# Gated units: turned rows placed a step earlier, moments and norms issued tile by tile

## The chip, the cores and the metric

The kernel runs on one core of one Trainium2 chip. A core has five engines that run side by side and wait for each other through semaphores: TensorE (PE in the profile; its weight loads are listed as PEld), VectorE (DVE), ScalarE (ACT), GpSimd (POOL) and SyncE (SP), which here issues most of the DMAs. The metric is the device time of one execution in microseconds (us); the time of a kernel is the median of several executions.

## What is computed

The reference takes x of shape (2, 2048, 256) in float32 and adds two sublayers to it, each between layer norms. The first is an attention of three branches. The second is a stack of two layers, and it is the one that matters here:

```python
def _layer(x, wqkv, qs, ksc, wo, lg, lb, w1, b1, w2, b2):
    h = shift_token(x)                      # second half of the channels from the token before
    q, k, v = split(h @ wqkv)               # 8 heads of 64
    q, k = rotary_xpos(l2norm(q) * qs, l2norm(k) * ksc)
    x = x + local_attention(q, k, v) @ wo   # window of 128, one window back
    h = shift_token(x)
    mu, var = h.mean(-1), h.var(-1)
    h = (h - mu) / sqrt(var + 1e-05) * lg + lb
    a, g = split(h @ w1 + b1)               # 682 columns each
    x = x + (a * gelu(g)) @ w2 + b2
    return x
for l in range(2):
    x = _layer(x, ...)
```

The change touches the last five lines of a layer, which the kernel calls the gated units.

## The kernel before

**Tiling.** A tile is 128 tokens (on the 128 partitions) by 256 channels; there are 16 tiles in each of the 2 batches. Four tiles (GT) make a group, so there are 8 groups, X[g] holds the input and Y[g] the running value of a group in SBUF. Attention runs tile by tile, 32 a layer, the batches taking turns. The gated units run group by group, 8 a layer, the batches taking turns too (GORDER). The 682 hidden columns are cut into six chunks (NCH): five of 128 and one of 42.

**An order written out by hand.** Nothing is reordered by a planner. Every piece of work is put on a list with a place (`put(place, f, ...)`), the list is sorted by place, and the functions are called in that order. Each engine carries out its own instructions in the order of the calls. A tile of attention comes every 12400 places (TILE), a chunk of the gated units every 5170 (STEP). A place is only a rank: an instruction starts when its engine has come to it and what it waits for is done. Where an item and a chunk have the same step, the chunk's products come first (offset 0), then its gate (offset 10), then the item (offset 20).

**A gated group.** For group i the steps count from its first chunk. `shift` (step -9) brings the second half of the channels down by one token: two DMAs on SP's queue from Y into `sh`, one more for row 0 from the last token of the group before (`kept`, copied by POOL; for the first group of a batch POOL writes zeros). `moments` (step -6) takes mean and variance of the four tiles (`stats`: two L149 and one L150 on VectorE a tile) and the inverse deviation (`rstd_of`, L155 and L156 on POOL). `normed` (steps -4 and -3) writes the normed halves `hn` (L160, four a half, VectorE); with the second half POOL adds the second bias to Y (L1036). `turned` (steps -2 and -1) turns a half with four TensorE transposes into one PSUM bank (L1042) and scales it into `hT` (L1043, VectorE). `inner` (steps 0 to 5) multiplies hT by a chunk of w1 (L1051): a gate product and a value product, each over two halves of the contraction; the last, narrow chunk has both in one. `gate` takes the Gelu on ScalarE (L1069) and the product with the value on VectorE (L1070) into `u`. `back` (steps 6 to 9, beside the next group's chunks 0 to 3) multiplies u by w2 (L1077) and adds to Y (L1079). In the second layer `closing_moments` and `closing_norm` follow half a step and one and a half steps after each back, and SP stores the rows (L1092).

**Where stages meet.** The gated units of a layer start before its attention ends: step 0 of group 0 stands 28150 places after the start of the last tile, and until place 37400 after it no Gelu is called. So the last tiles' attention (L924 divides the probabilities, L934 turns them, L976 sums the two parts of the output, L981 projects it, L810, L821, L828, L832 and L836 prepare queries and keys) stands among the first two groups' shifts, moments, norms and turns. `sh` and attention's output `oT` share two buffers; so do attention's `rr` and the gated units' hn and hT (`hh`). PSUM has two banks each for pa and pb and four for pc. The place of the steps is in one line, and it is what the change edits:

```python
plan += [(-9, shift), (-6, moments), (-4, normed, 0), (-3, normed, 1), (-2, turned, 0), (-1, turned, 1)]
...
for i, g in enumerate(GORDER):
    for c in range(NCH):
        place = base + (NCH * i + c) * STEP
        put(place, inner, g, c, ...)
        put(max(place, no_gate_until) + 10, gate, g, c)
    for at, f, *arg in plan:
        put(base + (NCH * i + at) * STEP + 20, f, g, *arg)
```

## Time and profile before

| what | us |
|---|---|
| median of 3 runs (1682.47 to 1685.27) | 1682.78 |
| the profiled execution | 1687.03 |
| its span, first to last instruction | 1685.3 |
| TensorE clock granted, mean | 0.98 of full |
| gated units, first layer: from one group to the next in mid-stage | 31.50 |
| L1051, product of a chunk with w1, one instruction (mean) | 0.61 |
| L1042, transposes in the gated units, one (mean) | 0.28 |
| L1043, scaling of a turned half, one (mean) | 0.81 |
| L160, norm of a half tile, one (mean of each half) | 0.34 and 0.43 |

A span runs from the first to the last instruction that the profiler saw; 1.7 us of the profiled execution lie around it. In the timelines, matmuls are pipelined: consecutive ones overlap, so the time from one start to the next says more than a duration. The slices of the span show the stages:

```profile
PE   5999985699999999879999999999999997999998
DVE  2555566478888788843333336888888885344443
POOL 6401245575665666611110146666666662123322
```

Each digit is the busy share of an engine in one of 40 equal slices of 42 us, in tenths. Slices 0 to 6 are the first sublayer; 7 to 16 attention of the first layer and 17 to 22 its gated units; 23 to 33 and 34 to 39 the same of the second layer. In the gated units TensorE is nearly always busy and VectorE and GpSimd are not. In attention three engines are busy.

### The profile page before, as it was taken

The numbers are of one execution on the slowest core, as the hardware profiler recorded it, in microseconds if no ns is written. First come the engines' busy times: TensorE is split into PE (matmuls) and PEld (weight loads), VectorE is DVE, ScalarE is ACT, GpSimd is POOL, SyncE is SP. The second block draws the span as 40 slices with busy tenths as digits, with TensorE's granted clock in tenths as the row PEclk, the third lists the DMA queues.
The fourth block names the chain that finished last, engine by engine and source line by source line (L and its number), as shares of the span: only waits on it lengthen the run. The fifth ranks groups of instructions, "written<-read, shape, count | busy, mean of one in ns | idle before, by whom it ended". The sixth has DMA issues, their size and how long they took to land.

```text
span 1685.3 us, 32263 instructions
## 1 busy us (share of the span) xinstructions
PE 1560.2 (93%) x12255; PEld 1034.6 (61%) x12255; DVE 1044.4 (62%) x3084; ACT 757.7 (45%) x2201; POOL 748.2 (44%) x932
## 2 busy tenths in 40 slices
PE   5999985699999999879999999999999997999998
PEld 4966763266666666645555556666666664555555
DVE  2555566478888788843333336888888885344443
ACT  3334364367677677531111125767767763111110
POOL 6401245575665666611110146666666662123322
PEclk9999997899999999999999999999999998999999
DMA  6000000200000000011000001000000000000000
GB/s 204 2 1 1 1 1 0 78 8 5 8 8 6 8 8 8 6 47 26 9 7 16 0 32 29 8 8 5 8 8 5 10 3 13 8 24 27 26 26 25
DMA packets 31674, 30.40 MB, mean 18 GB/s; under 512 B 4344, under 2 KB 29792, under 8 KB 31520
## 3 DMA queue, kind: packets, MB, share of 16 engines
q1 hardware_dynamic: 27264, 25.17, 4.7%
q10 hardware_dynamic: 3200, 2.63, 0.5%
q8 instruction: 97, 1.59, 0.4%
q0 software_dynamic: 1056, 0.55, 0.4%
q14 instruction: 57, 0.47, 0.1%
HBM read 19.95 MB, written 4.19 MB: 14 GB/s over the span
## 4 chain that ended last, share of the span: by engine, by line
PE 71%; DVE 5%; ACT 1%; POOL 1%; DMA 1%; issue 1%; POOLq 0%; SPq 0%; DVEq 0%; ACTq 0%
PE pa L794 18%; PE pc L1077 10%; PE pa L1051 9%; PE pb L1051 7%; PE pb L981 6%; PE pb L934 5%; PE pc L954 5%; PE pc L887 5%; PE pb L844 3%; PE pc L1051 1%; DMA sh<-Y 1%; DVE hh L1043 1%; DVE u L1070 1%; DVE rr L810 1%; PE pb L772 1%; DVE hh L160 1%
## 5 line engine op out<-in xcount | busy, mean ns | idle before, releaser
L794 PE MATMUL pa<-wqkv,h 128*128 128x512 f32 x768 | 373.6, 609 | 21.6 <-ACT h L776 10.3
L821 POOL TENSOR_TENSOR rr<-rr 128x256 f32<-128x256 f32 x256 | 178.8, 732 | 301.2 <-DVE rr L810 267.1
L1069 ACT ACTIVATE ge<-pa,vcol 128x512 f32<-128x512 f32 x92 | 62.9, 686 | 384.8 <-PE pa L1051 384.8
L917 ACT ACTIVATE prob<-prob,off 128x192 f32<-128x192 f32 (+2 forms) x512 | 225.0, 443 | 15.4 <-DVE off L908 14.8
L794 PEld LDWEIGHTS pa<-wqkv,h 128*128 128x128 f32 x768 | 132.1, 192 | 134.2 <-issue 104.7
L155 POOL TENSOR_SCALAR r<-mv 128x1 f32<-128x1 f32 (+2 forms) x72 | 15.8, 219 | 446.2 <-DVE mv L150 445.4
L1051 PE MATMUL pa<-hh,w 128*128 128x512 f32 x368 | 182.3, 613 | 20.9 <-DVE hh L1043 15.6
L832 POOL TENSOR_TENSOR ss<-ss,mhalf 128x16 f32<-128x16 f32 x64 | 186.5, 2914 | 5.3 <-DVE den L922 4.0
L939 ACT COPY probT<-pb 128x384 f32<-128x384 f32 (+1 forms) x256 | 119.7, 468 | 149.0 <-PE pb L934 145.9
L1077 PE MATMUL pc<-w,u 128*128 128x256 f32 x768 | 176.3, 380 | 0.0
L1077 PEld LDWEIGHTS pc<-w,u 128*128 128x128 f32 x768 | 146.4, 191 | 46.1 <-issue 29.3
L810 DVE TENSOR_TENSOR rr<-pa,cs 128x1024 f32<-128x1024 f32 x128 | 150.5, 1215 | 19.4 <-POOL cs L765 14.4
L904 DVE CUSTOM_DVE_ANT_0 prob<-pc,mask_loc 128x192 f32<-128x192 f32 (+2 forms) x512 | 148.6, 345 | 19.9 <-PE pc L887 19.1
L1070 DVE SCALAR_TENSOR_TENSOR u<-pb,vcol,ge 128x512 f32<-128x512 f32 x73 | 54.7, 749 | 152.3 <-PE pb L1051 133.2
L1051 PE MATMUL pb<-hh,w 128*128 128x512 f32 x292 | 138.3, 596 | 0.0
L934 PE MATMUL pb<-ident,prob 128*128 128x128 f32 x752 | 119.7, 282 | 18.6 <-DVE prob L924 16.7
L934 PEld LDWEIGHTS pb<-ident,prob 128*128 128x128 f32 x752 | 90.7, 144 | 72.6 <-issue 39.9
L836 POOL TENSOR_TENSOR rr<-rr,ss 128x512 f32<-128x512 f32 x128 | 131.5, 1048 | 2.5
L924 DVE TENSOR_TENSOR prob<-prob,den 128x768 f32<-128x768 f32 x128 | 127.3, 995 | 5.0
L981 PE MATMUL pb<-wo,oT 128*128 128x256 f32 x512 | 122.9, 383 | 5.3 <-DVE oT L976 4.1
L801 ACT ACTIVATE sq<-pa 128x512 f32<-128x512 f32 x128 | 75.8, 592 | 94.6 <-PE pa L794 91.8
L887 PE MATMUL pc<-kr,qT 64*64 64x192 f32 (+2 forms) x2688 | 111.9, 290 | 3.6 <-ACT qT L848 3.3
(263 smaller groups left out, 2549.5 us busy)
## 6 DMA issues: line engine op xcount, KB each, us to landing
X<-_attn_hidden_states_dram SPq DMA_DIRECT2D x8, 512.0 KB
cs<-in_rope_dram SPq DMA_DIRECT2D x32, 128.0 KB
out_dram<-res SPq DMA_DIRECT2D x32, 128.0 KB
sh<-Y SPq DMA_DIRECT2D x16, 254.0 KB
w<-in_L_ffn_w_dram SPq DMA_DIRECT2D x6, 640.0 KB
wqkv<-in_L_ffn_wqkv_dram SPq DMA_DIRECT2D x2, 1536.0 KB
Wc<-in_L_attn_Wc_dram ACTq DMA_DIRECT2D x1, 1024.0 KB
wo<-in_L_ffn_wo_dram SPq DMA_DIRECT2D x2, 512.0 KB
```

The source lines that it names most:

```text
L794: nc.tensor.matmul(ps, lhsT=src, rhs=W[l]["wqkv"][:, h, j * INNER : (j + 1) * INNER], start=(h == 0), stop=(h == 1))
L810: nc.vector.tensor_tensor(s["rr"][:, j], ps, tab, ALU.mult)
L821: nc.gpsimd.tensor_tensor(dst, dst, rr[:, j, 1, :, hi : hi + hd], ALU.add)
L832: nc.gpsimd.tensor_tensor(S[n]["ss"], S[n]["ss"], mhalf, ALU.pow)
L836: nc.gpsimd.tensor_tensor(dst, dst, S[n]["ss"][:, j * HEADS : (j + 1) * HEADS].unsqueeze(2).to_broadcast([P, HEADS, DH]), ALU.mult)
L887: nc.tensor.matmul(ps[half][at : at + HALF, i, c : c + m], lhsT=s["qT"][lo : lo + DH, pair, half * HALF : (half + 1) * HALF], rhs=KR[b][lo ...
L904: nc.vector.tensor_tensor_reduce(out=p[:, i, half, lo:hi], in0=s["s", quad][half][:, i, lo:hi], in1=mask_loc[:, lo:hi], scale=1.0, scalar= ...
L917: nc.scalar.activation(ph, ph, AF.Exp, bias=s["off", quad][:, j : j + 1], accum_out=s["den", quad][:, j : j + 1])
L934: nc.tensor.transpose(pt[:, c, :], flat[:, c * P : (c + 1) * P], ident)
L981: nc.tensor.matmul(pz, lhsT=S[n]["oT"][:, i, :], rhs=W[l]["wo"][:, i, :], start=(i == 0), stop=(i == HEADS // 2 - 1))
L1051: nc.tensor.matmul(ps, lhsT=w1_s[:, h, lo : lo + P], rhs=s["hT"][:, h, :], start=(h == 0), stop=(h == 1))
L1077: nc.tensor.matmul(pz, lhsT=s["u"][:, c, k * P : (k + 1) * P], rhs=W[l]["w2"][:, c, :], start=(c == 0), stop=(c == NCH - 1))
```

## The change

`moments` is cut into four calls of one tile each, at steps -7, -6.78, -6.56 and -6.34; the inverse deviation stays at step -6 in a call of its own, `deviations`. `normed` is cut into eight calls of one tile and half, from step -4.5 to -2.96 at 0.22 of a step; the buffer `hh` is asked for in the first of them. The second bias is a call of its own at step -2.5. The two turns go from -2 and -1 to -2.1 and -1.1. With the offset of 20 places, -2 and -1 came just after the chunk of that step; -2.1 and -1.1 come 497 places ahead of it (0.1 of a step less the offset). `shift` stays at -9. No arithmetic is changed.

```diff
-        def moments(g):
+        def moments(g, k):
             s = G[g]
-            mv = small.tile([P, GT, 2], F32, tag="mv4", name="mv")
-            for k in range(GT):
-                stats(mv[:, k, :], Y[g][:, k, 0:P], s["sh"][:, k, :])
-            s.update(mv=mv, r=rstd_of(mv, GT, 1e-5))
-            hh = act.tile([P, 2, 2 * GT * P], F32, tag="rr", name="hh")
-            s["hn"] = hh[:, 0].rearrange("p (h k t) -> p h k t", h=2, k=GT)
-            s["hT"] = hh[:, 1].rearrange("p (h t) -> p h t", h=2)
-
-        def normed(g, h):
+            if k == 0:
+                s["mv"] = small.tile([P, GT, 2], F32, tag="mv4", name="mv")
+            stats(s["mv"][:, k, :], Y[g][:, k, 0:P], s["sh"][:, k, :])
+
+        def deviations(g):
+            G[g]["r"] = rstd_of(G[g]["mv"], GT, 1e-5)
+
+        def normed(g, h, k):
             s = G[g]
-            for k in range(GT):
-                norm(s["hn"][:, h, k, :], s["sh"][:, k, :] if h else Y[g][:, k, 0:P], s["mv"], k, s["r"])
-            if h:
-                nc.gpsimd.tensor_tensor(Y[g], Y[g], W[l]["b2"].unsqueeze(1).to_broadcast([P, GT, H]), ALU.add)
+            if "hn" not in s:
+                hh = act.tile([P, 2, 2 * GT * P], F32, tag="rr", name="hh")
+                s["hn"] = hh[:, 0].rearrange("p (h k t) -> p h k t", h=2, k=GT)
+                s["hT"] = hh[:, 1].rearrange("p (h t) -> p h t", h=2)
+            norm(s["hn"][:, h, k, :], s["sh"][:, k, :] if h else Y[g][:, k, 0:P], s["mv"], k, s["r"])
+
+        def second_bias(g):
+            nc.gpsimd.tensor_tensor(Y[g], Y[g], W[l]["b2"].unsqueeze(1).to_broadcast([P, GT, H]), ALU.add)
...
         plan = [(NCH + k, back, k) for k in range(GT)]
-        plan += [(-9, shift), (-6, moments), (-4, normed, 0), (-3, normed, 1), (-2, turned, 0), (-1, turned, 1)]
+        plan += [(-9, shift), (-6, deviations), (-2.5, second_bias), (-2.1, turned, 0), (-1.1, turned, 1)]
+        plan += [(-7 + 0.22 * k, moments, k) for k in range(GT)]
+        plan += [(-4.5 + 0.22 * (h * GT + k), normed, h, k) for h in range(2) for k in range(GT)]
```

## The prediction

> **What bounds the kernel now.** I read the page first (busy shares, slices), then who TensorE waits for, then the timelines of TensorE, VectorE, GpSimd and the DMA queue in a group of gated units in mid-stage and in the overlap where attention ends.

> ```profile
> PE 1560.2 (93%) x12255; PEld 1034.6 (61%) x12255; DVE 1044.4 (62%) x3084; ACT 757.7 (45%) x2201; POOL 748.2 (44%) x932
> ```

> and from the list of waits (total us, times, longest):

> ```profile
> PE pa L1051 <- DVE hh L1043: 15.6, 14, 1.2
> PE pb L981 <- DVE oT L976: 4.1, 3, 1.5
> ```

> TensorE is the bound, 93% busy. Of its waits only one comes back in every group: 14 times (groups 2 to 8 of each layer) the first gate product waits for L1043, the scaling that takes the turned rows out of PSUM. TensorE in a mid group:

> ```profile
> 882.29 1.88 PE L1051 MATMUL pa<-hh,w 128*128 128x512 f32 x4
> 884.00 1.88 PE L1051 MATMUL pb<-hh,w 128*128 128x512 f32 x4
> 885.72 0.60 PE L1042 MATMUL pc<-ident,hh 128*128 128x128 f32 x4
> 886.16 1.88 PE L1051 MATMUL pa<-hh,w 128*128 128x512 f32 x4
> 887.88 0.60 PE L1042 MATMUL pc<-ident,hh 128*128 128x128 f32 x4
> 888.31 1.02 PE L1051 MATMUL pa<-hh,w 128*128 128x512 f32 x2
> 890.44 1.12 PE L1051 MATMUL pa<-hh,w 128*128 128x512 f32 x2 [1.11 <-DVE hh L1043]
> 891.40 1.88 PE L1051 MATMUL pb<-hh,w 128*128 128x512 f32 x4
> ```

> Chunk 4 (two products), first turn, chunk 5 (one product), second turn, then the next group's chunk 0: its first half needs only the first turned half and runs, its second half waits. VectorE at that time:

> ```profile
> 886.66 0.80 DVE L1043 TENSOR_SCALAR hh<-pc,vcol 128x512 f32<-128x512 f32 x1
> 888.79 0.75 DVE L1070 SCALAR_TENSOR_TENSOR u<-pa,vcol,ge 42x512 f32<-42x512 f32 x1 [1.33 <-ACT ge L1069]
> 889.58 0.81 DVE L1043 TENSOR_SCALAR hh<-pc,vcol 128x512 f32<-128x512 f32 x1
> ```

> The second turn is done at 888.31, but its L1043 stands in VectorE's queue behind chunk 5's gate product, which waits for ScalarE. It ends at 890.39 and TensorE goes on at 890.44.

> In the overlap of layer one (676 to 767; layer two repeats it at 1362 to 1452) other things decide[...]. TensorE's waits there:

> ```profile
> 688.13 1.97 PE L981 MATMUL pb<-wo,oT 128*128 128x256 f32 x8 [1.08 <-DVE oT L976]
> 707.15 1.51 PE L934 MATMUL pb<-ident,prob 128*128 128x128 f32 x6 [4.25 <-DVE prob L924]
> 717.49 1.99 PE L981 MATMUL pb<-wo,oT 128*128 128x256 f32 x8 [1.50 <-DVE oT L976]
> ```

> VectorE's rows that stand before them, then GpSimd's, then the DMA queue's issue and VectorE's read of what it brings:

> ```profile
> 701.58 3.94 DVE L160 TENSOR_SCALAR hh<-sh,mv,r 128x128 f32<-128x128 f32 x4
> 744.12 2.78 DVE L924 TENSOR_TENSOR prob<-prob,den 128x768 f32<-128x768 f32 x1
> ```

> ```profile
> 702.84 2.34 POOL L1036 TENSOR_TENSOR Y<-Y,b 128x1024 f32<-128x1024 f32 x1
> ```

> ```profile
> 706.38 0.71 SPq L1016 DMA_DIRECT2D sh<-Y  x1
> ```

> ```profile
> 721.43 0.29 DVE L149 BATCH_NORM_STATS2 st<-sh 128x6 f32<-128x128 f32 x1 [0.21 <-DMA sh<-Y]
> ```

> Four norms that elsewhere take 1.10 us take 3.94, and L924 takes 2.78 for 0.96, each time beside POOL's second bias. The shifted rows (sh), issued from 705.59, are there at 721.4: some 15.8 us.

> [...]L924 ends 0.8 after L1036 does (746.09). [...]254 KB in 15 us is 17 GB/s, so I expect these 15 us wherever sh is issued. [...]After 4.25 us idle the six transposes at 707.15 take 1.51; the same six take 0.82 at 691.98.

> **The change part by part.**

> *Turns a step sooner.* Place -1.1 puts the second turn ahead of chunk 5, and its L1043 ahead of chunk 5's gate product on VectorE; the first one goes ahead of chunk 4. Take chunk 4's end as 0. Second turn until 0.43. VectorE has chunk 4's gate product from 0.27 to 1.02 (885.99 against 885.72), then L1043 from 0.94 to 1.75. TensorE needs it after chunk 5 (1.72) and the half product (0.86): at 0.43 + 1.72 + 0.86 = 3.01. It is 1.2 early; no wait is left. What goes: the product would have started at 888.31 + 0.86 = 889.17 and started at 890.44: 1.27, plus 0.10 since it restarts slower (0.96 to the next one instead of 0.86). 1.37 a group. Check: five chunks at 3.44, 1.72, four backs at 2.59 and two turns at 0.43 make 30.14; the groups stand 31.50 apart (854.82, 886.32, 917.82 in the chain of waits). 14 x 1.37 = 19.2 us off. In the second layer a closing norm (place -1.5), perhaps held by the second bias, delays L1043 by some 0.7: still 0.6 early.

> *Norms in pieces* (64 of each half, 0.34 us; none added). In mid-stage nothing waits for them. They straddle the shift of the next group (-9), so that sh's old buffer is still in use there and the other one is taken. In layer one the DMA queue then no longer waits for the norms of the group before (issue at 884.00, norms done 883.93): it can issue much sooner. The second bias (POOL, 2.35 us) starts as soon as the first half's last norm is done and nothing of POOL's own is ahead[...]; the gate product of chunk 3 behind it is asked for 3.44 + 0.27 after that back's sum and has over 5 us until its bank is needed: nothing. The buffer of hn and hT is asked for at the first norm instead of at the moments; the attention tiles that share it are asked for in the same order as before: nothing.

> *Moments a step sooner, in pieces* (each 0.63: two L149, one L150). They now come right after chunk 5's gate product. In layer two the sh DMAs stand behind an output store (1597.28, then 1597.70) and land at about 1614.1; The store waits for a closing norm that comes 0.5 sooner (two norms ahead of it instead of four, 0.26 apart), so 1613.6. VectorE gets to the moments at about 1607 and blocks there over 6 us. Queued behind: the gate products of chunks 0 and 1 and a back's sum. The moments end at 1613.6 + 0.46 + 3 x 0.63 = 1616.0, chunk 0's gate product (0.75) at 1616.7, which is 11.3 after the group's first product (1605.41). TensorE needs that bank for chunk 2's second product at 2 x (3.44 + 2.59) + 1.72 = 13.8. Cover 2.4; cost nothing, and beyond it one for one. The price of this wait is bounded by 0 (sh landed) and by the whole landing time; I take the trace's 15.8 to 16.4 from issue.

> *Overlap, tiles 27 and 28.* Four moments stood in a block at 683.80 ahead of L976. Two of them now fall into VectorE's wait for scores (0.70 at 679.73)[...]; L976 comes 1.0 sooner, and the stall of 1.08 at 688.13 mostly goes: 0.9 off a layer.

> *Overlap, group 1.* Its norms spread out and the second bias moves behind L832: the 4.25 stall (L924 behind four norms and L828) shortens by about 2. On POOL the order was L821, second bias, the copy for the next shift, L832 (2.9), L836; now it is L821, copy, L832, second bias, L836: L832 starts at about 703.6 instead of 705.98, but with 2.9 and 2.35 before it L836 starts at about 708.9, as before (708.96), and TensorE's turn of those rows waits for it. I count 0; bounds -2 and +2.35. The second turn now stands ahead of three transposes of probabilities and waits for a bank that L972 frees: under 0.2.

> *Overlap, group 2.* Its sh takes the buffer that L981 of tile 28 frees (702.5; 701.7 with the 0.9 gained) instead of that of the norms (705.52), so it lands at 701.7 + 15.9 = 717.6. But its first moments now stand ahead of tile 29's L976, which was at 716.76 in front of them: 717.6 + 0.46 + 0.68 puts L981 at 718.85 instead of 717.49: 1.36 later. In layer two the same sum gives 1404.1 for 1401.95: 2.15. In layer one the idle time before it grows to over 4 us, so TensorE may come back at half clock[...]; in layer two L981 is already slow there (3.41). After it three norms are ahead of time, and the second bias starts 0.85 sooner against L924: 0.85 off a layer, and 0.3 (no wait for tops in layer one).
> Layer one: 1.36 + 1.7 - 0.85 - 0.3 = +1.9; layer two 2.15 - 0.85 = +1.3. (The 0.9 is inside these.) Bounds for both together: -3.5 if sh lands before it is asked for[...].

> Sum: -19.2 + 3.2 = -16. The profiled execution was 1687.03 (span 1685.3), so 1671 for its like; the median of the runs shown is 1682.78, 4.2 lower, and gives **1667**. About 0.2% (3.4 us) is what a measurement of this kernel can tell from no change.

> **Rivals.** *The overlap gives, too* (sh is not late): -19.2 - 3.5 = -22.7, 1660. For: one block of moments visibly stalls L981. Against: 15.8 us of DMA. *The wait moves to the moments in mid-stage*: sh comes later than worked out and eats the cover of 2.4; at 0.5 to 1 us in each of ten groups, 5 to 10 back: 1674. For: five waits of 0.4 to 0.5 us on sh are there today a step later. *Slower*: the same DMA in layer two decides the group. Five groups (4 to 8) lose one for one beyond 2.4; they eat the 16 at 3.2 each, so from 5.6 us later than I have it; at 7 us it is 5 x 4.6 = 23, 1690. For: output stores and sh share a queue, and some stores take 7.5 us to issue. Against: sh is issued before those. *It doesn't do what it says*: L1043 stays behind a late gate product, 1682.

> **How the numbers follow.** Forecast 0.60 (its own range 1661 to 1672), overlap gives 0.12, mid-stage wait 0.14, slower 0.10, nothing 0.04. Leaving out the last two and the outer part of the third: 1659 to 1675. Faster 0.86, same 0.04, slower 0.10.

> **What would show it.** Right: groups 30.1 us apart in both layers, no wait of L1051 for L1043; in layer two waits of VectorE's L149 for sh of about 6 us; L981 near 718.9 waiting behind sh. Wrong: groups still over 30.5 apart, L1051's second product waiting for L1070, or a gap over 6 us before L981 of tile 29.

## The result and the profile after

| | before | after |
|---|---|---|
| median of 6 runs, us | 1684.31 (1682.47 to 1685.27) | 1667.32 (1665.84 to 1671.76) |
| profiled execution; its span, us | 1687.03; 1685.3 | 1667.55; 1665.8 |
| from group to group in mid-stage, us | 31.50 | 30.12 |

The ratio is 0.9903, 95% interval 0.989 to 0.9916: 17 us faster, where 1667 had been forecast. In the changed kernel every line from the second bias on is three higher: turns L1045, scaling L1046, products L1054, Gelu L1072, gate product L1073, back L1080, second bias L1039, store L1095.

The page's busy times first (busy us, share of the span, instructions):

```profile
PE 1559.2 (94%) x12255; PEld 1038.1 (62%) x12255; DVE 1054.1 (63%) x3084; ACT 757.0 (45%) x2201; POOL 748.3 (45%) x932
```

TensorE works as long as before (1560.2); what went is idle time. Its list of waits (total us, times, longest) no longer has L1054 waiting for L1046 at all, where L1051 waited 14 times for L1043. Something else has grown: before, L844 waited 2.4 us in all for L836. L934 has come down from 16.7.

```profile
PE pb L844 <- POOL rr L836: 9.9, 5, 3.7
PE pb L934 <- DVE prob L924: 9.4, 5, 2.9
PE pb L981 <- DVE oT L976: 4.5, 2, 2.4
```

TensorE in the same mid group as the one shown of before (start, us, engine, line, operation, tiles, count):

```profile
876.68 0.60 PE L1045 MATMUL pc<-ident,hh 128*128 128x128 f32 x4
877.11 1.88 PE L1054 MATMUL pa<-hh,w 128*128 128x512 f32 x4
878.83 1.88 PE L1054 MATMUL pb<-hh,w 128*128 128x512 f32 x4
880.55 0.60 PE L1045 MATMUL pc<-ident,hh 128*128 128x128 f32 x4
880.99 3.60 PE L1054 MATMUL pa<-hh,w 128*128 128x512 f32 x8
```

First turn, chunk 4, second turn, then eight products in one unbroken row: chunk 5 and both halves of the next group's chunk 0. And VectorE beside it:

```profile
880.82 0.75 DVE L1073 SCALAR_TENSOR_TENSOR u<-pb,vcol,ge 128x512 f32<-128x512 f32 x1 [2.54 <-PE pc L1045]
881.49 0.80 DVE L1046 TENSOR_SCALAR hh<-pc,vcol 128x512 f32<-128x512 f32 x1
883.62 0.75 DVE L1073 SCALAR_TENSOR_TENSOR u<-pa,vcol,ge 42x512 f32<-42x512 f32 x1 [1.33 <-ACT ge L1072]
```

L1046 now stands between chunk 4's gate product and chunk 5's. It ends at 882.29; TensorE comes to the half that needs it at 880.55 + 3.01 = 883.56, 1.3 us later.

In the overlap of layer one TensorE's waits have changed places:

```profile
702.62 0.85 PE L934 MATMUL pb<-ident,prob 128*128 128x128 f32 x6 [1.56 <-DVE prob L924]
...
708.61 1.12 PE L844 MATMUL pb<-ident,rr 128*128 128x128 f32 x4 [3.73 <-POOL rr L836]
710.40 1.11 PE L844 MATMUL pb<-ident,rr 128*128 128x128 f32 x4 [0.67 <-POOL rr L836]
711.44 2.64 PE L954 MATMUL pc<-probT,v 64*64 64x128 f32 x64
...
718.13 1.99 PE L981 MATMUL pb<-wo,oT 128*128 128x256 f32 x8 [2.37 <-DVE oT L976]
```

The stop of 4.25 us before L934 is down to 1.56, but 3.73 and 0.67 us of waiting for GpSimd's L836 stand right behind it, and L981 waits longer than before (1.50). GpSimd shows why L836 is no sooner: the second bias stands ahead of it.

```profile
701.53 3.71 POOL L832 TENSOR_TENSOR ss<-ss,mhalf 128x16 f32<-128x16 f32 x1
705.22 2.33 POOL L1039 TENSOR_TENSOR Y<-Y,b 128x1024 f32<-128x1024 f32 x1
707.52 2.83 POOL L836 TENSOR_TENSOR rr<-rr,ss 128x512 f32<-128x512 f32 x2
```

The same in the kernel before, whose execution is 0.7 us behind at the start of the overlap:

```profile
708.96 2.05 POOL L836 TENSOR_TENSOR rr<-rr,ss 128x512 f32<-128x512 f32 x2
```

To compare kernels, I cut the execution at TensorE's own instructions: the overlap from L981 of tile 25 to the first back of the third group (it holds three of the seven waits a layer), and mid-stage from there to the first back of the eighth group (the other four).

| us | overlap, layer 1 | mid-stage 1 | overlap, layer 2 | mid-stage 2 |
|---|---|---|---|---|
| before | 168.5 | 169.1 | 168.8 | 151.8 |
| after | 165.0 | 163.6 | 166.3 | 146.3 |

Mid-stage gives 4 x 1.375 in each layer. The overlaps should give 3 x 1.375 = 4.1; they give 3.5 and 2.6, so they cost 0.6 and 1.6 us. A last 1.6 us comes from the hand-over to layer two, where four projections run at full clock after and not before (1.98 us for 3.12). The stretch from the eighth group's first back to L981 of the fifth tile of layer two takes 81.0 to 81.1 us in eight of the fourteen profiled kernels and 82.7 to 82.8 in the other six, and kernels with the whole change stand among both. The pieces alone are among the eight, the turns alone among the six. The clock decides there, as the last section shows for six of them: this gain is not the change's.

### The profile page after: what moved, and what is told of

The parts are those of the page before. It is cut to its first block, busy times and chain, and to the rows that moved or that the text cites. A ratio compares the mean times of both kernels' runs of the same rounds, so it can differ in the third digit from the quotient of the medians.

```text
span 1665.8 us, 32261 instructions
## 1 busy us (share of the span) xinstructions
PE 1559.2 (94%) x12255; PEld 1038.1 (62%) x12255; DVE 1054.1 (63%) x3084; ACT 757.0 (45%) x2201; POOL 748.3 (45%) x932
## 3 DMA queue, kind: packets, MB, share of 16 engines
q8 instruction: 97, 1.59, 0.4%
## 4 chain that ended last, share of the span: by engine, by line
PE 84%; DVE 7%; POOL 4%; DMA 3%; ACT 1%; issue 1%; SPq 0%; POOLq 0%; ACTq 0%; DVEq 0%
PE pa L794 19%; PE pc L1080 10%; PE pa L1054 10%; PE pb L1054 8%; PE pb L981 6%; PE pc L954 5%; PE pb L934 5%; PE pc L887 5%; PE pb L844 3%; DMA sh<-Y 2%; PE pc L317 1%; DVE st L149 1%; PE pc L1054 1%; PE pa L442 1%; PE pa L545 1%
## 5 line engine op out<-in xcount | busy, mean ns | idle before, releaser
L821 POOL TENSOR_TENSOR rr<-rr 128x256 f32<-128x256 f32 x256 | 177.8, 727 | 303.6 <-DVE rr L810 273.0
L1072 ACT ACTIVATE ge<-pa,vcol 128x512 f32<-128x512 f32 x92 | 62.9, 686 | 366.6 <-PE pa L1054 355.9
L832 POOL TENSOR_TENSOR ss<-ss,mhalf 128x16 f32<-128x16 f32 x64 | 188.1, 2939 | 3.6 <-DVE den L922 2.3
L1054 PE MATMUL pa<-hh,w 128*128 128x512 f32 x368 | 176.4, 609 | 5.3 <-ACT ge L1072 5.3
L1080 PE MATMUL pc<-w,u 128*128 128x256 f32 x768 | 175.8, 379 | 0.0
L1080 PEld LDWEIGHTS pc<-w,u 128*128 128x128 f32 x768 | 146.2, 190 | 45.0 <-issue 28.6
L1054 PE MATMUL pb<-hh,w 128*128 128x512 f32 x292 | 139.2, 599 | 0.0
L836 POOL TENSOR_TENSOR rr<-rr,ss 128x512 f32<-128x512 f32 x128 | 132.9, 1058 | 2.4
L924 DVE TENSOR_TENSOR prob<-prob,den 128x768 f32<-128x768 f32 x128 | 127.8, 998 | 4.9
L934 PEld LDWEIGHTS pb<-ident,prob 128*128 128x128 f32 x752 | 89.5, 142 | 65.2 <-DVE prob L924 27.7
L934 PE MATMUL pb<-ident,prob 128*128 128x128 f32 x752 | 118.1, 279 | 11.2 <-DVE prob L924 9.4
L981 PE MATMUL pb<-wo,oT 128*128 128x256 f32 x512 | 123.1, 384 | 4.5 <-DVE oT L976 4.5
L1073 DVE SCALAR_TENSOR_TENSOR u<-pb,vcol,ge 128x512 f32<-128x512 f32 x73 | 54.7, 750 | 111.0 <-PE pb L1054 85.2
```

Source lines behind the costliest of these rows:

```text
L821: nc.gpsimd.tensor_tensor(dst, dst, rr[:, j, 1, :, hi : hi + hd], ALU.add)
L832: nc.gpsimd.tensor_tensor(S[n]["ss"], S[n]["ss"], mhalf, ALU.pow)
L836: nc.gpsimd.tensor_tensor(dst, dst, S[n]["ss"][:, j * HEADS : (j + 1) * HEADS].unsqueeze(2).to_broadcast([P, HEADS, DH]), ALU.mult)
L934: nc.tensor.transpose(pt[:, c, :], flat[:, c * P : (c + 1) * P], ident)
L981: nc.tensor.matmul(pz, lhsT=S[n]["oT"][:, i, :], rhs=W[l]["wo"][:, i, :], start=(i == 0), stop=(i == HEADS // 2 - 1))
L1054: nc.tensor.matmul(ps, lhsT=w1_s[:, h, lo : lo + P], rhs=s["hT"][:, h, :], start=(h == 0), stop=(h == 1))
```

## The experiments

### Which part carries the gain

The turns alone, in the kernel before:

```diff
-(-2, turned, 0), (-1, turned, 1)
+(-2.1, turned, 0), (-1.1, turned, 1)
```

> The kernel before with nothing but the two turns moved (places -2.1 and -1.1); moments, norms and second bias stay as they were. Theory (the turns carry the whole gain, the pieces none of it): groups 30.1 us apart, no wait of L1051 for L1043, 14 x 1.37 = 19.2 us off, and without the 2.2 us by which the two traces show the overlaps dearer after the full change: 1684.3 - 19.2 = 1665 us (1663 to 1667). Rival (the pieces keep VectorE's queue short and carry part of it): groups 30.5 or more apart, 1672 us or more.

Measured: 1665.62 us (1664.87 to 1667.63), ratio 0.9894 (0.9879 to 0.9908); groups 30.12 apart, no wait of L1051 for L1043. The turns carry the whole gain: 17.8 us in the medians, and 14 x 1.375 = 19.25 in the trace, which the interval (15.5 to 20.4 us) doesn't tell apart. Overlaps 164.3 and 164.5: both give the 4.1 and a little more.

The pieces alone, the same edit undone in the changed kernel:

```diff
-(-2.1, turned, 0), (-1.1, turned, 1)
+(-2, turned, 0), (-1, turned, 1)
```

> The changed kernel with the two turns put back to -2 and -1; moments and norms stay in pieces and the second bias on its own. Theory: the wait of L1054 for L1046 is back, 14 times 1.1 us, groups 31.5 apart, and the overlaps cost some 2 us: 1686 us (1684 to 1688). Rival (pieces carry part of the gain): 1680 us or less, groups under 31.3 apart.

Measured: 1687.75 us (1684.22 to 1693.26, 17 runs), ratio 1.0022 (1.0014 to 1.0029), groups 31.50 apart. Its list of waits has the old one back:

```profile
PE pa L1054 <- DVE hh L1046: 15.6, 14, 1.2
```

The pieces bring nothing in mid-stage and cost in the overlaps (170.1 and 170.8 for 168.5 and 168.8), some 4 us in the medians. The rival is out.

The second turn alone, the first one left at -2:

```diff
-(-2, turned, 0), (-1, turned, 1)
+(-2, turned, 0), (-1.1, turned, 1)
```

> The kernel before with only the second turn moved (place -1.1), the first one at -2 as before: both turns then stand together ahead of chunk 5. Theory: the second half of the turned rows is ready 2.5 us after chunk 4's end (two scalings behind chunk 4's gate product) and asked for at 2 x 0.43 + 1.72 + 0.86 = 3.44: the whole gain, groups 30.1 apart, 1665 us (1663 to 1667). Rival (the first turn has to move too, or the two turns wait for each other's bank): groups 30.4 or more apart, 1669 us or more.

Measured: 1665.03 us (1663.23 to 1665.63), ratio 0.9886 (0.9874 to 0.9899), groups 30.12 apart. One number of the diff, -1 to -1.1, is the whole gain: the turn moves by a tenth of a step, which is enough to put it ahead of a chunk.

And the cause tried from the other side, with TensorE's order as it was: only chunk 5's gate goes behind the second turn.

```diff
-put(max(place, no_gate_until) + 10, gate, g, c)
+put(max(place, no_gate_until) + (30 if c == NCH - 1 else 10), gate, g, c)
```

> The kernel before with only chunk 5's gate (activation and gate product) put behind the second turn in the order, so that L1043 stands ahead of L1070 on VectorE; TensorE's own order is untouched. Theory (what cost the time is L1043's place in VectorE's queue): L1043 starts about 0.1 us after the turn ends, and TensorE has only the half product (0.86 us) as cover for 0.81 us and two handovers: 0.24 us of stall and the 0.10 us of slower restart are left, groups 30.5 apart, 14 x 1.0 = 14 us off, 1670 us (1668 to 1673). Rival (what counts is that chunk 5's product stands between turn and use on TensorE): groups 31.2 or more apart, 1680 us or more.

Measured: 1668.48 us (1667.69 to 1669.19), ratio 0.9909 (0.9896 to 0.9921), groups 30.43 apart. VectorE in this kernel:

```profile
881.60 0.80 DVE L1043 TENSOR_SCALAR hh<-pc,vcol 128x512 f32<-128x512 f32 x1
883.46 0.81 DVE L1043 TENSOR_SCALAR hh<-pc,vcol 128x512 f32<-128x512 f32 x1 [1.05 <-PE pc L1042]
884.30 0.75 DVE L1070 SCALAR_TENSOR_TENSOR u<-pa,vcol,ge 42x512 f32<-42x512 f32 x1
```

The second L1043 now waits for TensorE's turn and not behind the gate product, which follows it. Of the 1.37 us a group, 1.07 are VectorE's queue; the last 0.31 need cover on TensorE. So the wait was one of order on VectorE, as argued.

### What the stop on sh costs in layer two

The changed kernel with the shift of layer two one place later, behind one more output store:

```diff
-(-9, shift)
+(-8 if l else -9, shift)
```

> The changed kernel with the shift of layer two one place later (-8 for -9; layer one untouched): the three DMAs of sh then stand behind one more output store. Theory (in layer two VectorE stands still on sh with a cover of 2.4 us for TensorE, beyond it one for one): the stores are some 6 us apart, so sh lands 6 us later in the five groups that follow stores, each loses 6.0 - 2.4 = 3.6 us, 18 us in all: 1685 us (1680 to 1690), groups 4 to 8 of layer two 33.7 apart, layer one still 30.1. Rival (VectorE has more slack than that, TensorE doesn't feel it): 1670 us or less.

Measured: 1691.61 us (1688.75 to 1691.71), ratio 1.0048 (1.0032 to 1.0063), slower than the kernel before and just above the expected range. Layer one keeps its 30.12; groups 4 to 8 of layer two begin 35.23, 33.50, 34.96, 33.60 and 36.54 after the group ahead of them. VectorE's wait for sh in one of them and the gate product behind it, first in the changed kernel, then with the late shift:

```profile
1596.91 0.29 DVE L149 BATCH_NORM_STATS2 st<-sh 128x6 f32<-128x128 f32 x1 [6.38 <-DMA sh<-Y]
...
1599.26 0.75 DVE L1073 SCALAR_TENSOR_TENSOR u<-pb,vcol,ge 128x512 f32<-128x512 f32 x1
```

```profile
1548.83 0.29 DVE L149 BATCH_NORM_STATS2 st<-sh 128x6 f32<-128x128 f32 x1 [12.04 <-DMA sh<-Y]
...
1551.18 0.75 DVE L1073 SCALAR_TENSOR_TENSOR u<-pb,vcol,ge 128x512 f32<-128x512 f32 x1
```

TensorE's waits there:

```profile
1518.45 1.98 PE L1054 MATMUL pb<-hh,w 128*128 128x512 f32 x4 [3.12 <-DVE u L1073]
1551.98 3.41 PE L1054 MATMUL pb<-hh,w 128*128 128x512 f32 x4 [3.14 <-DVE u L1073]
1587.01 1.98 PE L1054 MATMUL pb<-hh,w 128*128 128x512 f32 x4 [3.21 <-DVE u L1073]
```

In the five groups VectorE stands 5.7 to 5.8 us longer and TensorE waits 3.1 to 3.2. That is what a cover of 2.5 to 2.6, and one for one beyond it, would give; only this one lateness was tried. What the theory lacked is the restart: three of the five come back at half clock (3.41 to 3.78 for 1.98). The five groups lose 23.2 us, 15.9 of it this wait. Beyond the wait, the three that restart at half clock lose 1.7 to 3.2 us each, the other two 0.3.

### What makes the overlaps dearer

Three edits of the changed kernel, each alone. First the landing of sh, its DMA cut in two:

```diff
-nc.sync.dma_start(sh[1:P, :, :], y[0 : P - 1, :, P:H])
+nc.sync.dma_start(sh[1:113, :, :], y[0:112, :, P:H])
+nc.sync.dma_start(sh[113:P, :, :], y[112 : P - 1, :, P:H])
```

> The changed kernel with the DMA of 127 shifted partitions cut into one of 112 and one of 15. Theory[...]: sh is there 3 to 5 us after issue for 15.8, VectorE's waits of L149 for sh (32 us in layer two) shrink to under 5, the wait before L981 of tile 29 (2.4 us) goes in both overlaps, nothing in mid-stage: 1664 us (1662 to 1666). Rival (the landing is limited by something else, or another wait ends just as late in the overlap): landing over 10 us, or no gain: 1667 us.

Measured: 1664.76 us (1663.77 to 1669.67), ratio 0.9894 (0.9879 to 0.9909). The SP queue's issues:

```profile
701.53 0.77 SPq L1015 DMA_DIRECT2D sh<-Y  x1
702.35 0.65 SPq L1016 DMA_DIRECT2D sh<-Y  x1
703.05 0.88 SPq L1017 DMA_DIRECT2D sh<-Y  x1
```

By the medians on this run's page the 112 partitions land 3.0 us after their issue and the 15 after 4.0. The last of the three is issued 1.5 us after the first, so sh is there, by my estimate from these numbers, some 5.5 us after its first issue, for 15.8. What makes 127 partitions slower than 112 was not shown; the 3 to 5 us of the expectation were my estimate. VectorE's waits for sh (32.4 us in layer two) are gone from its list. But L981 still waits 1.77 and 1.76 us, for 2.37 and 2.12: L976 stands behind the second turn's scaling and one moment, sh or no sh. That part of the expectation missed. Against the changed kernel the gain of 2.6 us isn't certain from the times, whose intervals overlap.

Then the moments put back a step, still in pieces:

```diff
-(-6, deviations)
+(-5.2, deviations)
-(-7 + 0.22 * k, moments, k)
+(-6 + 0.22 * k, moments, k)
```

> The changed kernel with the moments put back by a step (-6 + 0.22 k for -7 + 0.22 k, deviations at -5.2), still in pieces. Theory (moving the moments a step sooner is what makes the overlap dearer, since they put VectorE on hold for sh ahead of tile 29's L976): the wait of 2.4 us before L981 goes, VectorE's waits for sh in layer two fall to under 1 us each, 1.4 to 2 us back in each layer: 1664 us (1662 to 1666). Rival (the norms and the second bias are what costs): 1667 us, L844's waits for L836 unchanged at some 9.9 us.

Measured: 1662.39 us (1659.96 to 1668.48), ratio 0.9884 (0.9866 to 0.9902). L981's waits fall to 1.17 in both layers, VectorE's for sh to 6.8 in all (five of 1.3 to 1.4, where under 1 had been expected); L844's stay (11.2). Overlaps 163.6 and 162.6. So moving the moments a step sooner brought nothing, and in these two executions it cost 1.4 and 3.7 us in the two overlaps. Of this 1.2 and 1.0 us are L981's wait; in layer two most of the rest are two restarts at full clock for half (L981 1.99 us for 3.55, L1054 1.98 for 3.36). The times alone don't settle it: the intervals just overlap, and the five executions spread over 8.5 us.

Last the second bias, behind both L836:

```diff
-(-2.5, second_bias)
+(-1.9, second_bias)
```

> The changed kernel with the second bias at -1.9 for -2.5, in the overlap behind both L836 of the last tile. Theory (the second bias, 2.3 us on GpSimd ahead of L836, is what L844 waits for in the overlap, 9.9 us in all against 2.4 before): L844's waits fall to 5 us or less, 2 us less in each overlap: 1663 us (1661 to 1666). Rival (L924, or the stop on sh, ends just as late): the wait moves there, 1667 us.

Measured: 1669.49 us (1668.53 to 1671.33), ratio 0.9917 (0.9904 to 0.9931). TensorE's waits in the overlap of layer one:

```profile
705.03 0.66 PE L844 MATMUL pb<-ident,rr 128*128 128x128 f32 x4 [1.53 <-POOL rr L836]
706.04 0.66 PE L844 MATMUL pb<-ident,rr 128*128 128x128 f32 x4 [0.34 <-POOL rr L836]
716.74 3.78 PE L981 MATMUL pb<-wo,oT 128*128 128x256 f32 x8 [6.88 <-DVE oT L976]
```

L844's waits fall to 5.0 us as the theory had it, but the time doesn't fall with them (it is 2 us higher, with intervals that overlap): the rival's case. TensorE gets to L981 sooner, and waits there for sh, which lands when it did; VectorE shows it:

```profile
715.60 0.29 DVE L149 BATCH_NORM_STATS2 st<-sh 128x6 f32<-128x128 f32 x1 [5.01 <-DMA sh<-Y]
716.05 0.63 DVE L976 TENSOR_TENSOR oT<-oT,pc 128x512 f32<-128x512 f32 x1
```

If that is so, the two edits together must give what neither gives alone:

```diff
-(-2.5, second_bias)
+(-1.9, second_bias)
-nc.sync.dma_start(sh[1:P, :, :], y[0 : P - 1, :, P:H])
+nc.sync.dma_start(sh[1:113, :, :], y[0:112, :, P:H])
+nc.sync.dma_start(sh[113:P, :, :], y[112 : P - 1, :, P:H])
```

> The changed kernel with both the later second bias (-1.9) and the shift's DMA cut in 112 and 15 partitions. Theory (the later bias does free TensorE, but VectorE's stop on sh, 5.0 us there, then stands ahead of L976 and ends last; with sh landed in 3 us nothing is in its place): L981's wait of 6.9 us falls to about 1, and its half clock goes: 5 to 6.5 us less in each overlap than with the later bias alone (1669.5): 1657 us (1655 to 1661). Rival (L976 is late for another reason, the second turn or L924 under the bias): 1665 us or more.

Measured: 1659.28 us (1655.31 to 1659.35), ratio 0.9841 (0.9823 to 0.9859): 10 us less than the later bias alone, with L981's waits at 1.76 and 1.77. In the traces 3.9 and 5.1 us of that lie in the overlaps, where 5 to 6.5 had been expected, and 1.8 at the hand-over, as far apart as the two lengths given for it above. That settles it: the two waits end close together, and only both edits free TensorE. The half clock after L981 stayed (3.28 and 3.54 us for 1.99), hence the upper part of the expected range.

The other pair removes one stop twice; the same cut of the DMA, and

```diff
-(-6, deviations)
+(-5.2, deviations)
-(-7 + 0.22 * k, moments, k)
+(-6 + 0.22 * k, moments, k)
```

> The changed kernel with the shift's DMA cut in two and the moments put back by a step. Theory (the two edits remove the same stop of VectorE on sh): no more than the moments put back alone, 1662 us (1660 to 1664), with VectorE's waits for sh gone. Rival (they add up, 2.5 us from the landing and 5 us from the moments): 1660 us or less.

Measured: 1665.19 us (1663.97 to 1667.76), ratio 0.9884 (0.9866 to 0.9901): above the expected range in the median, with the ratio of the moments put back alone. The waits are those of the moments put back alone (L981 1.17 and 1.17, L844 10.4 in all). What differs is the clock after equal waits. Moments put back alone:

```profile
736.81 1.98 PE L1054 MATMUL pa<-hh,w 128*128 128x512 f32 x4 [2.64 <-ACT ge L1072]
```

With the DMA cut too:

```profile
736.95 3.68 PE L1055 MATMUL pa<-hh,w 128*128 128x512 f32 x4 [2.64 <-ACT ge L1073]
```

The same again in layer two (3.56 for 1.98), and 1.7 us at the hand-over. The edits do not add up. That the profiled execution of the pair is longer is nothing that its waits show.

### A version that beats both

All three edits; to the cut of the DMA come

```diff
-(-6, deviations), (-2.5, second_bias)
+(-5.2, deviations), (-1.9, second_bias)
-(-7 + 0.22 * k, moments, k)
+(-6 + 0.22 * k, moments, k)
```

> The changed kernel with all three edits: later second bias, the DMA cut in two, moments put back by a step. Theory: like the later bias with the cut DMA, and L976 has no moment ahead of it, 0.6 us in each layer: 1656 us (1654 to 1660). Rival (the moments, a step later, run into the norms or the bias of the same group): 1660 us or more.

Measured: 1655.42 us (1655.1 to 1658.33), ratio 0.9828 (0.9811 to 0.9845): 28 us under the kernel before, 12 under the changed one. Overlaps 159.7 and 159.9, mid-stage unchanged. The later bias with the cut DMA had 161.6 and 162.4; 0.6 us of each difference is L981's wait, most of the rest its restart (1.99 for 3.28 and 3.54). TensorE's waits in the overlap of layer one:

```profile
707.11 0.66 PE L844 MATMUL pb<-ident,rr 128*128 128x128 f32 x4 [1.54 <-POOL rr L836]
...
714.69 1.99 PE L981 MATMUL pb<-wo,oT 128*128 128x256 f32 x8 [1.17 <-DVE oT L976]
```

With the first turn back at -2 as well:

```diff
-(-2.1, turned, 0)
+(-2, turned, 0)
```

> The same three edits, and the first turn back at -2 behind chunk 4. Theory (the second turn alone carries the steady gain): groups 30.1 apart as with both turns moved, and in the overlap 0 to 1.4 us less: 1655 us (1653 to 1659). Rival: groups over 30.3 apart or 1660 us and more.

Measured: 1657.89 us (1656.61 to 1658.85), ratio 0.9838 (0.9822 to 0.9855), groups 30.12 apart, overlaps 159.8 and 160.0. No further gain, against the expectation, and no loss that these runs tell from none: the first turn didn't have to move.

## Why the prediction held, step by step

- **Turns, -19.2.** Right in place, cause and size: 14 x 1.375 = 19.25, shown by the turns alone and by the second turn alone. The scaling was put 1.2 us early and is 1.3. The first turn's move, which the change also makes, isn't needed.
- **Moments in layer two, cost 0 with a cover of 2.4.** Right: VectorE stands 6.4 us on sh, chunk 0's gate product ends 11.4 after the group's first product (worked out: 11.3), and TensorE asks for its bank 13.8 after it. The late shift fits the cover (2.5 to 2.6) and the price beyond it. So the slower rival was a real road: sh 5.7 us later costs more than the whole gain. Its price was too low, by the restarts at half clock.
- **Tiles 27 and 28, 0.9 gained.** Right: L981 of tile 27 doesn't wait; 1.1 in layer one, 0.7 in layer two.
- **Group 1, counted 0.** The mechanism was right: 4.25 goes, L836 ends no sooner than before behind the bias (in layer one it starts 0.7 us sooner against the rest, and takes 2.83 for 2.05 beside an L924 of 1.68 us, 0.96 elsewhere), and L844 waits for it. The size was not: from L981 of tile 28 to its wait in tile 29 TensorE takes 1.6 us longer in layer one and 2.9 in layer two. That uses up the gain of tile 27 and leaves it 0.5 and 2.1 us later than before, inside the bound of 2.35. L954 comes back at half clock behind the new wait of 3.73 (2.64 for 1.57 before; in layer two 2.84 for 1.59), and in layer two L844 itself had run at full clock before (1.11 for eight, 1.91 in layer one). That the half clock moves along with the wait was missing from this term.
- **Group 2, +1.36 and +2.15 for L981 of tile 29.** By the trace it comes 1.36 and 2.74 later, both counted from L981 of tile 25. The numbers written down for layer one, 717.6 + 0.46 + 0.68, make 718.74 and not 718.85, so +1.25. The reason given for the earlier issue was wrong: sh didn't take the buffer that L981 of tile 28 frees. GpSimd's row for sh waits for L160, the last norm of the group before, and SP follows at 701.14; the norms end sooner because they are spread. The number (701.7) came out nearly right from the wrong premise. The landing was right: 15.85 us from issue to VectorE's read at 716.99. But VectorE waits only 0.50 and 0.25 us for it there: the second turn, late by what group 1 lost, ends nearly as late, and so L981 kept most of its wait with the faster landing.
- **Half clock after L981 in layer one, 1.7.** The size was my estimate; no trace shows it. The half clock didn't come (1.99 for eight products after 2.37 us idle). In layer two it did (3.55), as before (3.41).
- **Regained at L924, 0.85 a layer, and 0.3.** L934 comes 0.86 sooner in both layers (2.94 of waiting for 3.80). Layer two keeps it; in layer one it was given back at once, since the clock there is at half for 6.8 us (3.4 before), and the eight products behind it take 3.62 and 2.07 us for 2.91 and 1.88. The 0.3 was 0.7.
- **Layer one's queue "can issue much sooner".** Wrong, without effect: sh is issued at 787.27, when the last norm on the sh of two groups earlier has ended at 787.20, as in the kernel before (884.00 after 883.93); the two buffers take turns in both kernels.

The overlaps' sum was forecast as +1.9 and +1.3 and is +0.6 and +1.6. In layer one two errors of the clock offset each other, the half clock that didn't come (1.7) and the 0.85 that didn't stay; in layer two L981's 0.6 more is in part made up by small gains. That the sum is near is in part luck. So is a hit within 0.3 us: the forecast of -16 started from a median of 1682.78, and from the later 1684.31 it would have given 1668; measured are -17.0. What made it safe is that these terms are small beside 19.2, which was read from a stage where one wait comes back 14 times.

Open: what the norms in pieces cost on their own was not tried. How much of each overlap term is half clock can't be taken apart from the edits, since it changes with equal waits, and one execution of each kernel is read here.

## What to carry to other kernels

A short operation whose result TensorE waits for must not stand behind one that waits for a third engine; look at the queue order of the consumer's engine, not only at TensorE's. Here one place by a tenth of a step gave the whole gain, and the rest of the edit gave a little of it back. Where two waits end close together, removing one shows the other: the later bias alone gained nothing, and together with the faster landing it is 8 us better than the changed kernel, so such edits are worth trying in pairs before one is dropped.

## What the runs showed of the hardware

The clock after a wait isn't set by that wait's length alone. The wait of 2.64 us before the first product with a Gelu behind it is the same in 14 profiled kernels and both layers; the four products after it take 1.98 us in 8 of 28 cases, and 2.56 to 3.68 in the others. At the hand-over to layer two six kernels (before, after, and the first four of the runs above) have the same wait of 0.63 us, behind two close ahead of it (0.68, and 0.39 or 0.40 us; of the second turn alone only the 0.63 is shown); the four products after the last take 1.98 us in three of them (after, the pieces alone, chunk 5's gate behind the turn) and 3.12 to 3.42 in the other three. Before and after:

```profile
1012.53 3.12 PE L794 MATMUL pa<-wqkv,h 128*128 128x512 f32 x4 [0.63 <-DVE rr L810]
1002.80 1.98 PE L794 MATMUL pa<-wqkv,h 128*128 128x512 f32 x4 [0.63 <-DVE rr L810]
```

L981 of tile 29 waits 1.50 us in both layers of the kernel before. In layer one it comes back at full clock (1.99), in layer two at half:

```profile
1401.95 3.41 PE L981 MATMUL pb<-wo,oT 128*128 128x256 f32 x8 [1.50 <-DVE oT L976]
```

The clock records of the kernels before and after show more. In each of the two executions all 23 changes of the granted clock from 60 us on stand whole multiples of 3.41 us apart (before, 712.87 and 1402.36 are 202 steps apart; after, 713.74 and 1389.58 are 198), and this grid begins 2.90 us after the first instruction in the one and 0.35 in the other. The four grid windows around these two waits (stretch, its length, busy us and instructions of PE, PEld, DVE, ACT and POOL, then TensorE's granted clock, DMA share and GB/s):

```profile
712.87:716.28 3.41, 3.12 (x104) 2.81 (x103) 1.74 (x7) 1.81 (x4) 0.00 (x0) 1.00 0.09 26
716.28:719.69 3.41, 2.20 (x12) 1.95 (x13) 1.32 (x3) 1.60 (x8) 0.00 (x0) 1.00 0.07 21
1398.95:1402.36 3.41, 1.67 (x25) 1.30 (x18) 1.80 (x3) 2.49 (x10) 0.00 (x0) 1.00 0.09 26
1402.36:1405.77 3.41, 3.41 (x11) 2.68 (x10) 0.37 (x2) 0.00 (x0) 0.00 (x0) 0.50 0.07 21
```

Half clock needed no long wait: 1.50 us with 0.24 beside it, or the three short waits of the hand-over, were enough, and after 3.12 and 3.21 us with the late shift the clock stayed full (1.98 us for the four products). A restart at half clock cost 0.6 to 1.8 us in the products right behind, and 3.2 in the last of the late groups, where the twelve products of the back behind it were slow too (3.94 us for 2.75). So two kernels with nearly the same waits differ by 5 us here (spans of 1660.6 and 1665.8 with the moments put back, without and with the cut DMA).
